# Attention layer of a four-layer graph network: keys on partitions, no row maximum, sums from a product with ones

## The chip, the core and the metric

The kernel runs on one core of a Trainium2 chip. The metric is device time in microseconds (us) of one execution. A core has a matrix engine (PE, whose weight loads are shown as PEld), a vector engine (DVE), an activation engine (ACT), a general engine (POOL), and a queue engine that issues most transfers (SP). Each works through its own list of instructions; semaphores make one wait for another. PE writes to PSUM banks, and DVE or ACT read them from there.

## The reference, cut to what matters

There are 64 graphs of 256 nodes with 256 features, and four layers, each followed by a residual sum and a layer norm. Layer 0 is a recurrence over the nodes of all graphs at once. Layers 1 to 3 work on one graph after the other. Layer 3 is the one that is changed: attention with 8 heads of 32 features, masked by the adjacency matrix.

```python
x = _layernorm(x + L0(x, adj)); x = _layernorm(x + L1(x, adj)); x = _layernorm(x + L2(x, adj))
q = split_heads(x @ Wq + bq)
k = split_heads(x @ Wk + bk)
v = split_heads(x @ Wv + bv)
scores = jnp.einsum('bhqd,bhkd->bhqk', q, k) / np.float32(np.sqrt(HD))
scores = jnp.where(adj[:, None, :, :] > 0, scores, jnp.float32(NEG))
attn = jax.nn.softmax(scores, axis=-1)
out = jnp.einsum('bhqk,bhkd->bhqd', attn, v)
out = out.transpose(0, 2, 1, 3).reshape(b, n, D_OUT)
x = _layernorm(x + out @ Wo + bo)
```

## The kernel before

`_recurrence` computes layer 0 and leaves its result in DRAM (`Hd`). It takes the first 1.6 ms and isn't touched.

`_layers` computes layers 1 to 3. All of a graph's matrices are 256 x 256 and are held as tiles of 128 partitions x 2 x 256 in f32. The class `Graph` has one method for each step. Helpers do the recurring work:

- `flipped` (L923) transposes such a matrix on PE in four 128x128 pieces into a PSUM bank; ACT or DVE copies it out.
- `product` (L933) multiplies two such matrices with four matmuls of 256 columns into a bank.
- `norm_a` (L891) takes mean and variance on DVE (two `bn_stats`, two `bn_aggr`, one add) and the power -0.5 on POOL. Then either `norm_b` (L903) applies them with two DVE operations, or `norm_s` (L910) does it with a small DVE operation for the shift and two ACT operations.
- `row_max` (L950) adds a mask and takes the row's maximum on DVE; `row_exp` (L957) takes the exponential on ACT with that maximum as bias, and the row's sum beside it.

Layer 3 goes: `s3` multiplies queries (stationary) by keys for four heads at once, one half of the heads at a time (`hc` 0 or 1), into four PSUM banks of their own (`sc0` to `sc3`), with queries on partitions. For each head, `max3` and `exp3` make the softmax's numerators, `flip3` transposes them, so that keys lie on partitions, and `pT3` copies them to SBUF. `weights_a` and `weights_b` bring the inverse sums, spread over a head's features, into the same layout by two more transposes. `o3` multiplies by the values, four heads side by side in one bank, and scales with the inverse sums; `f3` is the output product.

The order of the work is written out by hand. In the string `ROUND` (L1197) a step such as `D.flip3.0` calls the method `flip3(0)` of the graph that is in stage D. There are six stages, L, A, B, C, D and E, and a graph moves on by one stage in each round. So a round holds one graph's worth of work, spread over six graphs. The loop at L1209 writes the rounds one after the other, and each engine gets its instructions in that order. Graphs are loaded two rounds ahead on SP. All flips, products and `o3` share a ring of four banks (tag `mm`, L920), taken in turn.

In `ROUND`, flips of attention heads (`D.flip3`) stand between steps that depend on each other, as in `B.xT.2 D.flip3.0 ... B.qk2.0`.

Of the kernel before, what the change touches and what calls it, by code (L numbers as in the profile page):

```python
# [15 lines left out]
NEG = 9000000000000000.0  # L16
EPS = 1e-5
FMAX = 3.0e38
P = 128


# [824 lines left out]
        flush(N - T // 2, N)  # L846


def _layers(tc, ident, Hd, x, adj, w1, b1, l2, l3, out):

# [7 lines left out]
    with ExitStack() as ctx:  # L860
# [9 lines left out]
            _load_col(nc, cols[:, s, :], b)  # L870
        mhalf = const.tile([P, 2], F32, name="mhalf")
        nc.gpsimd.memset(mhalf, -0.5)
        with tc.tile_pool(name="l_setup", bufs=1) as tmp, tc.tile_pool(
            name="l_setup_ps", bufs=2, space=bass.MemoryType.PSUM
        ) as tps:
            _load_wT(nc, tmp, tps, w1, ident, lambda c: W1T[:, :, c * P:(c + 1) * P], "w1")

            bv = tmp.tile([P, 2, P], F32, name="bv3")
            nc.vector.tensor_copy(bv, cols[:, 4, :].unsqueeze(2).to_broadcast([P, 2, P]))
            pb = tps.tile([P, D], F32, tag="wt", name="bv3_ps")  # L880
            for k in range(2):
                nc.tensor.matmul(pb, bv[:, k, :], W3["o"][:, k, :], start=(k == 0), stop=(k == 1))
            nc.vector.tensor_add(b3_r, b3_r, pb)
# [16 lines left out]
            nc.gpsimd.tensor_tensor(rstd, rstd, mhalf, ALU.pow)  # L900
            return mv, rstd

        def norm_b(y, mv, rstd):  # L903
            for c in range(2):
                nc.vector.tensor_scalar(
                    y[:, c, :], y[:, c, :], mv[:, c, 0:1], rstd[:, c:c + 1],
                    ALU.subtract, ALU.mult,
                )

        def norm_s(y, mv, rstd, t):  # L910

            shift = small.tile([P, 2], F32, tag="shift", name=f"shift_{t}")
            nc.vector.scalar_tensor_tensor(shift, mv[:, :, 0], -1.0, rstd, ALU.mult, ALU.mult)  # L913
            for c in range(2):
                nc.scalar.activation(
                    y[:, c, :], y[:, c, :], AF.Identity, bias=shift[:, c:c + 1],
                    scale=rstd[:, c:c + 1],
                )
# [44 lines left out]
        class Graph:  # L963


            def __init__(self, b):
                self.b = b

            def load(self):
                b = self.b  # L970
# [11 lines left out]
            def norm_a(self, l):  # L982
                self.mv = norm_a(self.y, f"{l}_{self.b}")

            def norm_b(self):
                norm_b(self.y, *self.mv)

            def norm_s(self, l):
                norm_s(self.y, *self.mv, f"{l}_{self.b}")


            def degrees_a(self):
# [13 lines left out]

            def adT(self):
                pt = flipped(self.ad, f"ad_{self.b}")
                self.adT_sb = new("adT", self.b)
                for c in range(2):  # L1010
                    nc.scalar.activation(  # L1011
                        self.adT_sb[:, c, :], pt[:, c, :], AF.Copy, scale=self.dis[:, c:c + 1]
                    )
# [21 lines left out]
            def masks(self):  # L1035
                self.neg2 = new("neg2", self.b)
                nc.gpsimd.tensor_scalar(self.neg2, self.ad, -1.0, NEG, ALU.add, ALU.mult)
                self.neg3 = new("neg3", self.b, 4)
                nc.gpsimd.tensor_scalar(self.neg3, self.ad, 0.0, -NEG, ALU.is_le, ALU.mult)

            def qk2(self, s):
                pm = product(W2["qk"[s]], self.xT_sb, f"2{s}_{self.b}")
# [5 lines left out]
            def v2(self):  # L1048
                pm = product(W2["v"], self.xT_sb, f"2v_{self.b}")
                self.vT2 = new("vT2", self.b)  # L1050
                for c in range(2):
                    nc.vector.tensor_scalar(
                        self.vT2[:, c, :], pm[:, c, :], cols[:, 5, c:c + 1], 0.0, ALU.add, ALU.max
                    )

            def w2(self):

                pm = product(self.vT2, W2["o"], f"2w_{self.b}")
                self.w2_sb = new("w2", self.b)
                nc.vector.tensor_copy(self.w2_sb, pm)  # L1060

            def s2(self):
                b = self.b
# [36 lines left out]
                setattr(self, f"qk3{s}", m)  # L1100

            def bias_3(self):
                nc.gpsimd.tensor_add(self.y, self.y, rows(b3_r))  # L1103

            def v3(self):
                pm = product(self.xT_sb, W3["v"], f"3v_{self.b}")
                self.v3_sb = new("v3", self.b)
                nc.vector.tensor_copy(self.v3_sb, pm)
                self.oT3 = new("oT3", self.b)
                self.sm, self.pT = {}, {}  # L1110
                self.mx3 = [None] * 2
                self.sums3 = [None] * 2

            def s3(self, hc):

                self.s_ps = [
                    ps.tile([P, 2, N], F32, tag=f"sc{i}", name=f"s3_{self.b}_{hc}_{i}", bufs=1)
                    for i in range(G)
                ]
                for c in range(2):  # L1120
                    for i in range(G):
                        r = slice(i * HD, (i + 1) * HD)
                        nc.tensor.matmul(  # L1123
                            self.s_ps[i][:, c, :], self.qk30[r, hc, c * P:(c + 1) * P],
                            self.qk31[r, hc, :], start=True, stop=True,
                        )

            def max3(self, h):
                hc, i = divmod(h, G)
                if i == 0:  # L1130
                    self.mx3[hc] = small.tile([P, G, 2], F32, tag="mx3", name=f"mx3_{self.b}_{hc}")
                    self.sums3[hc] = small.tile(
                        [P, 2, G], F32, tag="sums3", name=f"sums3_{self.b}_{hc}"
                    )
                self.sm[h] = new("sm3", f"{self.b}_{h}", 5)
                for c in range(2):
                    row_max(
                        self.sm[h], self.s_ps[i], self.neg3, c, ISQ, self.mx3[hc][:, i, c:c + 1]
                    )

            def exp3(self, h):
                hc, i = divmod(h, G)
                for c in range(2):
                    row_exp(
                        self.sm[h], c, self.mx3[hc][:, i, c:c + 1], self.sums3[hc][:, c, i:i + 1]
                    )

            def flip3(self, h):
                self.pT_ps = flipped(self.sm[h], f"p3_{self.b}_{h}")

            def pT3(self, h):
                self.pT[h] = new("pT3", f"{self.b}_{h}", 8)
                (nc.vector.tensor_copy if h % G == G - 1 else nc.scalar.copy)(  # L1153
                    self.pT[h], self.pT_ps
                )

            def weights_a(self, hc):

                nc.vector.reciprocal(self.sums3[hc], self.sums3[hc])  # L1159
                self.rw = new("rw", f"{self.b}_{hc}", shape=(P, 2, G, HD))  # L1160
                nc.gpsimd.tensor_copy(  # L1161
                    self.rw, self.sums3[hc].unsqueeze(3).to_broadcast([P, 2, G, HD])
                )

            def weights_b(self, hc):
                r_ps = bank(f"tr_r_{self.b}_{hc}", (P, N))
                for c in range(2):
                    nc.tensor.transpose(
                        r_ps[:, c * P:(c + 1) * P], self.rw[:, c].rearrange("p g d -> p (g d)"),
                        ident,  # L1170
                    )
                self.rT = new("rT", f"{self.b}_{hc}", shape=(P, N))
                nc.scalar.copy(self.rT, r_ps)

            def o3(self, hc):

                o_ps = bank(f"o3_{self.b}_{hc}", (P, N))
                for k in range(2):
                    for i in range(G):
                        h = hc * G + i  # L1180
                        nc.tensor.matmul(  # L1181
                            o_ps[i * HD:(i + 1) * HD], self.v3_sb[:, k, h * HD:(h + 1) * HD],
                            self.pT[h][:, k, :], start=(k == 0), stop=(k == 1),
                        )
                nc.vector.tensor_mul(self.oT3[:, hc, :], o_ps, self.rT)

            def f3(self):
                pm = product(self.oT3, W3["o"], f"3f_{self.b}")
# [4 lines left out]

        ROUND = """  # L1197
            B.xT.2 D.flip3.0 D.exp3.1 D.pT3.0 B.qk2.0 D.max3.2 C.norm_a.2 A.norm_s.0 L.residual_0
            D.flip3.1 D.exp3.2 E.weights_b.1 D.pT3.1 E.o3.1 B.qk2.1 D.max3.3 C.norm_b B.masks B.v2
            D.flip3.2 D.exp3.3 D.pT3.2 E.f3 D.s3.1 A.xT.1 D.max3.4 C.xT.3 C.bias_3 E.norm_a.3  # L1200
            D.flip3.3 D.exp3.4 D.pT3.3 B.s2 D.weights_a.0 C.qk3.0 D.max3.5
            D.flip3.4 D.exp3.5 D.pT3.4 D.weights_b.0 A.t C.qk3.1 B.exp2 D.max3.6 E.norm_s.3 E.store L.degrees_a
            D.flip3.5 D.exp3.6 D.pT3.5 D.o3.0 A.g B.w2 D.max3.7 B.pT2 L.norm_a.0 L.degrees_b
            D.flip3.6 D.exp3.7 D.pT3.6 A.norm_a.1 C.v3 C.s3.0 C.max3.0 A.norm_b C.max3.1
            D.flip3.7 C.exp3.0 D.pT3.7 D.weights_a.1 L.adT B.f2
        """.split()
        graphs = [Graph(b) for b in range(B)]
        graphs[0].load()
        for t in range(-1, B + 4):  # L1209
            if 0 <= t + 2 < B:  # L1210
                graphs[t + 2].load()
            for step in ROUND:
                who, name, *args = step.split(".")
                b = t - "LABCDE".index(who) + 1
                if 0 <= b < B:
                    getattr(graphs[b], name)(*map(int, args))


@with_exitstack
def kernel(ctx: ExitStack, tc: tile.TileContext, ins, out):  # L1220
# [14 lines left out]
    l2, l3 = (  # L1235
        {w + n: ins[f"{l}_gnn_{w}{n}"] for w in "Wb" for n in "vkqo"} for l in ("L2", "L3")
    )
    _layers(tc, ident, Hd, x, adj, ins["L1_gnn_W"], ins["L1_gnn_b"], l2, l3, out)


# [34 lines left out]
```

## Time and profile before

| what | value |
|---|---|
| median of 3 runs | 3787.27 us (3783.76 to 3795.49) |
| the profiled execution | 3796.41 us |
| its span, first to last instruction | 3794.7 us |
| mean granted PE clock | 0.976 |
| instructions | 85826 |
| row maxima, L952, DVE | 1152 x 415 to 423 ns |
| exponentials, L959, ACT | 1152 x 502 ns, and as many reads of the sum, 192 ns |
| copies of flipped heads, L1153 | ACT 384 x 573 ns, DVE 128 x 682 ns |
| layer norm by `norm_b`, DVE / by `norm_s`, ACT | 256 x 423 ns / 256 x 593 ns |
| mask for layer 3, L1039, POOL | 1947 ns a graph |

A line of the page's groups reads: source line, engine, operation, output and input by name, sizes, count; then busy time in us, mean ns of one, and the idle time of the engine just before such an instruction, with what ended it. The table of windows gives busy time of each engine for a stretch of the span. The timeline lists instructions by start. The chain of waits follows the last instruction back to what released it, step by step.

### The profile page before, as it was taken

Reading aid. Unit: us, or ns where it says so; the run is one execution under the profiler, and the core shown is the slowest. Engines: PE = TensorE matmul, PEld = TensorE weight load, DVE = VectorE, ACT = ScalarE, POOL = GpSimd, SP = SyncE. Lnnn points to the kernel's source line nnn. Section 1 sums busy time; section 2 is a strip of 40 time slices with the busy share of each in tenths; the row PEclk is TensorE's granted clock in tenths of the full one; section 3 lists DMA queues with packets and bytes.
Section 4 is the critical chain, followed back from the end, with each engine's and each line's share of the span. In section 5 each row is a group of like instructions: output and inputs, shape, how many; then the busy total and the mean of one; then the engine's idle time right before and its main releaser. Section 6 shows DMA issues by size and latency. Waiting matters only on the chain.

```text
span 3794.7 us, 85826 instructions
## 1 busy us (share of the span) xinstructions
PE 3505.6 (92%) x31136; PEld 2546.6 (67%) x31136; DVE 2416.4 (64%) x8777; ACT 2020.5 (53%) x6307; POOL 1672.1 (44%) x1860
## 2 busy tenths in 40 slices
PE   6599999999999989679999999999999999999998
PEld 4355555555555555457777777777777777777776
DVE  1366666676667776446666666666666666666665
ACT  0144444444444444336666666666666666666666
POOL 2266666666667777333233333333333333333331
PEclk9799999999999999979999999999999999999999
DMA  8645575788875642320110011111101111110100
GB/s 286 190 142 137 144 178 133 184 193 200 199 178 148 165 128 74 74 69 26 34 34 29 29 34 34 34 34 34 31 26 34 34 34 34 34 34 26 33 18 15
DMA packets 380448, 331.96 MB, mean 87 GB/s; under 512 B 106220, under 2 KB 354168, under 8 KB 374904
## 3 DMA queue, kind: packets, MB, share of 16 engines
q1 hardware_dynamic: 358064, 307.05, 30.8%
q10 hardware_dynamic: 21960, 19.41, 1.5%
q8 instruction: 247, 4.05, 0.5%
q14 instruction: 177, 1.45, 0.1%
HBM read 224.01 MB, written 82.84 MB: 81 GB/s over the span
## 4 chain that ended last, share of the span: by engine, by line
PE 62%; DVE 20%; POOL 5%; DMA 5%; issue 4%; SPq 2%; ACT 1%; ACTq 0%; DVEq 0%; POOLq 0%
PE mm L938 9%; DVE sm L952 4%; PE rc L580 4%; PE rc L588 4%; PE tr_p L928 4%; PE mm_2v L938 3%; PE o L1181 3%; PE mm_g L938 3%; PE mm_t L938 3%; PE mm_2w L938 3%; PE mm_2s L938 3%; PE mm_3f L938 3%; DVE ACC L613 3%; PE late L504 3%; PE z_ps L580 2%
## 5 line engine op out<-in xcount | busy, mean ns | idle before, releaser
L959 ACT ACTIVATE sm<-sm,mx 128x256 f32<-128x256 f32 x1152 | 573.7, 502 | 165.5 <-DVE mx L952 159.2
L613 DVE SCALAR_TENSOR_TENSOR ACC<-keep,S,ACC 128x128 f32<-128x128 f32 x1712 | 504.4, 345 | 190.2 <-ACT hs L631 176.7
L952 DVE CUSTOM_DVE_ANT_0 sm<-s,neg 128x256 f32<-128x256 f32 x1024 | 386.5, 415 | 24.9 <-PE s L1123 24.9
L649 POOL TENSOR_TENSOR ACC<-ACC,far 128x384 f32<-128x384 f32 (+1 forms) x313 | 371.6, 1187 | 24.5
L928 PE MATMUL tr_p<-ident,sm 128*128 128x128 f32 x2304 | 344.1, 276 | 40.1 <-DVE sums L1159 36.0
L928 PEld LDWEIGHTS tr_p<-ident,sm 128*128 128x128 f32 x2304 | 271.7, 141 | 111.1 <-ACT adT L1011 48.5
L900 POOL TENSOR_TENSOR rstd<-rstd,mhalf 128x2 f32<-128x2 f32 x256 | 178.5, 697 | 357.9 <-DVE shift L913 188.9
L580 PE MATMUL rc<-WxT,xqT 128*64 128x256 f32 x2048 | 328.6, 400 | 1.0 <-issue 1.0
L645 POOL TENSOR_TENSOR far<-hs,S 128x384 f32<-128x384 f32 (+1 forms) x313 | 304.2, 972 | 4.7
L751 POOL TENSOR_TENSOR ready<-ACC,dinv 128x128 f32<-128x128 f32 x255 | 101.9, 400 | 424.8 <-DVE ACC L613 402.1
L1097 ACT ACTIVATE qk<-mm,b_cols 128x256 f32<-128x256 f32 x256 | 107.4, 471 | 267.2 <-PE mm L938 267.2
L1153 ACT COPY pT<-tr_p 128x512 f32<-128x512 f32 x384 | 219.9, 573 | 20.1 <-PE tr_p L928 20.1
L959 ACT ACTIVATION_READ_ACCUMULATOR sm<-sm,mx 128x1 f32 x1152 | 221.7, 192 | 0.0
L896 DVE BATCH_NORM_STATS2 st<-y 128x6 f32<-128x256 f32 x512 | 208.0, 406 | 3.7 <-POOL y L1032 3.6
L1018 ACT COPY xT<-tr_x 128x512 f32<-128x512 f32 x192 | 106.3, 588 | 186.0 <-PE tr_x L928 186.0
L597 ACT COPY xpT<-xpT_ps 128x128 f32<-128x128 f32 x256 | 68.1, 266 | 240.5 <-PE xpT_ps L595 240.5
L1103 POOL TENSOR_TENSOR y<-y,b3o_r 128x512 f32<-128x512 f32 x64 | 81.3, 1270 | 260.6 <-PE tr_x L928 258.8
L588 PE MATMUL rc<-WhT,xpT 128*64 128x128 f32 x2048 | 169.7, 287 | 28.1 <-ACT xpT L597 28.0
L1161 POOL COPY rw<-sums 128x256 f32<-128x256 f32 x128 | 50.7, 396 | 312.3 <-DVE sums L1159 312.1
L588 PEld LDWEIGHTS rc<-WhT,xpT 128*64 128x64 f32 x2048 | 107.4, 137 | 117.4 <-ACT xpT L597 84.2
L1000 POOL TENSOR_TENSOR dis<-dis,mhalf 128x2 f32<-128x2 f32 x64 | 44.2, 690 | 316.7 <-DVE dis L999 316.7
L1032 POOL TENSOR_TENSOR y<-y,g 128x512 f32<-128x512 f32 x64 | 81.4, 1273 | 228.8 <-ACT g L1029 224.4
(161 smaller groups left out, 8565.6 us busy)
## 6 DMA issues: line engine op xcount, KB each, us to landing
xX<-in_x_dram ACTq DMA_DIRECT2D x16, 1024.0 KB
Us<-xu SPq DMA_DIRECT2D x64, 256.0 KB
rows<-in_adj_dram SPq DMA_DIRECT2D x64, 256.0 KB
ACC<-Us SPq DMA_DIRECT2D x32, 512.0 KB
xq<-in_x_dram SPq DMA_DIRECT2D x64, 256.0 KB
Hw<-hs SPq DMA_DIRECT2D x512, 32.0 KB
Es<-eu SPq DMA_DIRECT2D x64, 256.0 KB
early_sb<-Es SPq DMA_DIRECT2D x32, 512.0 KB
```

The costliest lines, as they stand in the source:

```text
L580: nc.tensor.matmul(G[o * B:(o + 1) * B], xqT[a, i // 2][:, i % 2, kc, h * B:(h + 1) * B], WxT[:, kc, o, gates], start=False, stop=False, s ...
L588: nc.tensor.matmul(G[o * B:(o + 1) * B], hT[:, kc * B:(kc + 1) * B], WhT[:, kc, o, g], start=False, stop=(kc == 1), skip_group_check=True,)
L613: nc.vector.scalar_tensor_tensor(acc[:, 0, :], keep[:, j % 2, :], s, acc[:, 0, :], ALU.mult, ALU.add)
L645: nc.gpsimd.tensor_mul(tmp[:, 0:count, :], hs.unsqueeze(1).to_broadcast(shape), s.unsqueeze(2).to_broadcast(shape),)
L649: nc.gpsimd.tensor_add(acc, acc, tmp[:, 0:count, :])
L896: nc.vector.bn_stats(st, y[:, c, :])
L900: nc.gpsimd.tensor_tensor(rstd, rstd, mhalf, ALU.pow)
L928: nc.tensor.transpose(pt[:, a, c * P:(c + 1) * P], src[:, c, a * P:(a + 1) * P], ident)
L938: nc.tensor.matmul(pm[:, c, :], lhsT[:, k, c * P:(c + 1) * P], rhs[:, k, :], start=(k == 0), stop=(k == 1),)
L952: nc.vector.tensor_tensor_reduce(out=dst[:, c, :], in0=src[:, c, :], in1=neg[:, c, :], scale=-scale, scalar=FMAX, op0=ALU.add, op1=ALU.min ...
L959: nc.scalar.activation(dst[:, c, :], dst[:, c, :], AF.Exp, bias=mx, scale=-1.0, accum_out=sums)
L1153: (nc.vector.tensor_copy if h % G == G - 1 else nc.scalar.copy)(self.pT[h], self.pT_ps)
```

## The change

Layer 3 is rewritten from the scores on:

- `s3` makes keys the stationary operand, so the scores lie with keys on partitions, as the product with the values needs them. Then no head is flipped. For this the mask is needed transposed; `adT`, which has the transposed adjacency in PSUM already, makes it (`neg3`) on DVE. It was made by POOL in `masks`.
- The exponential is taken without the row's maximum: for each head DVE adds the mask to both halves at once (128x512), and ACT takes the exponential in place.
- `o3` multiplies the numerators by the values and again by a 128x32 tile of ones, into the other half of the bank. That gives each query's sum, spread over the head's 32 features. DVE inverts the sums (128x256), multiplies, and keeps the largest of sum + 1/sum in `far`.
- After the last graph, the largest of `far` is compared with `LIMIT`; all engines load the outcome and branch. If a sum was out of bounds, `_layer_3` computes the layer once more for all graphs, with the row's maximum. For that, `bias_3` stores the layer's input to DRAM (`Yd`).
- All layer norms are applied on ACT (the former `norm_s` is now `norm_b`). The evacuations of `v2`, `w2` and `v3` move from DVE to ACT.
- `ROUND` is written anew, with five stages and no `D`. `o3.0` is done in stage C and `o3.1` in stage E, one round later.

```diff
+LIMIT = 1.0e20
...
-def _layers(tc, ident, Hd, x, adj, w1, b1, l2, l3, out):
+def _layers(tc, ident, Hd, Yd, x, adj, w1, b1, l2, l3, out):
...
+        ones = const.tile([P, HD], F32, name="ones")
+        nc.gpsimd.memset(ones, 1.0)
+        far = const.tile([P, B, 2], F32, name="far")
...
-        def norm_b(y, mv, rstd):
-            for c in range(2):
-                nc.vector.tensor_scalar(
-                    y[:, c, :], y[:, c, :], mv[:, c, 0:1], rstd[:, c:c + 1],
-                    ALU.subtract, ALU.mult,
-                )
-
-        def norm_s(y, mv, rstd, t):
+        def norm_b(y, mv, rstd, t):
...
             def adT(self):
                 pt = flipped(self.ad, f"ad_{self.b}")
+
+                self.neg3 = new("neg3", self.b, 4)
+                nc.vector.tensor_scalar(self.neg3, pt, 0.0, -NEG, ALU.is_le, ALU.mult)
                 self.adT_sb = new("adT", self.b)
...
                 nc.gpsimd.tensor_scalar(self.neg2, self.ad, -1.0, NEG, ALU.add, ALU.mult)
-                self.neg3 = new("neg3", self.b, 4)
-                nc.gpsimd.tensor_scalar(self.neg3, self.ad, 0.0, -NEG, ALU.is_le, ALU.mult)
...
                 for c in range(2):
-                    nc.vector.tensor_scalar(
-                        self.vT2[:, c, :], pm[:, c, :], cols[:, 5, c:c + 1], 0.0, ALU.add, ALU.max
+                    nc.scalar.activation(
+                        self.vT2[:, c, :], pm[:, c, :], AF.Relu, bias=cols[:, 5, c:c + 1]
                     )
...
-                nc.vector.tensor_copy(self.w2_sb, pm)
+                nc.scalar.copy(self.w2_sb, pm)
...
             def bias_3(self):
+                nc.sync.dma_start(Yd[self.b], self.y)
                 nc.gpsimd.tensor_add(self.y, self.y, rows(b3_r))
...
-                nc.vector.tensor_copy(self.v3_sb, pm)
+                nc.scalar.copy(self.v3_sb, pm)
...
                         nc.tensor.matmul(
-                            self.s_ps[i][:, c, :], self.qk30[r, hc, c * P:(c + 1) * P],
-                            self.qk31[r, hc, :], start=True, stop=True,
+                            s_ps[i][:, c, :], self.qk31[r, hc, c * P:(c + 1) * P],
+                            self.qk30[r, hc, :], start=True, stop=True,
                         )
...
+                self.p = []
+                for i in range(G):
+                    p = new("p3", f"{self.b}_{hc}_{i}", 8)
+                    nc.vector.tensor_add(p, s_ps[i], self.neg3)
+                    nc.scalar.activation(p, p, AF.Exp, scale=ISQ)
+                    self.p.append(p)
+                self.ps_of[hc] = self.p
+
+            def o3(self, hc):
+
+
+                o_ps = bank(f"o3_{self.b}_{hc}")
+                for part in range(2):
+                    for k in range(2):
+                        for i in range(G):
+                            h = hc * G + i
+                            nc.tensor.matmul(
+                                o_ps[i * HD:(i + 1) * HD, part, :],
+                                ones if part else self.v3_sb[:, k, h * HD:(h + 1) * HD],
+                                self.ps_of[hc][i][:, k, :], start=(k == 0), stop=(k == 1),
+                            )
+                rT = new("rT", f"{self.b}_{hc}", shape=(P, N))
+                nc.vector.reciprocal(rT, o_ps[:, 1, :])
+                nc.vector.tensor_mul(self.oT3[:, hc, :], o_ps[:, 0, :], rT)
+                nc.vector.tensor_tensor_reduce(
+                    out=rT, in0=o_ps[:, 1, :], in1=rT, scale=1.0, scalar=0.0, op0=ALU.add,
+                    op1=ALU.max, accum_out=far[:, self.b, hc:hc + 1],
                 )
...
         ROUND = """
...
+            B.xT.2 C.norm_a.2 B.qk2.0 E.o3.1
+            B.qk2.1 C.norm_b.2 E.f3 B.masks L.residual_0
+            A.xT.1 B.v2 C.xT.3 C.bias_3 E.norm_a.3
+            B.s2 C.qk3.0 C.qk3.1 E.norm_b.3 E.store B.exp2
+            C.s3.0 A.t C.v3 B.w2 L.degrees_a
+            B.pT2 C.s3.1 A.g L.norm_a.0 L.degrees_b
+            B.f2 C.o3.0 A.norm_a.1 L.adT A.norm_b.1 L.norm_b.0
         """.split()
...
-        for t in range(-1, B + 4):
+        for t in range(-1, B + 3):
...
-                b = t - "LABCDE".index(who) + 1
+                b = t - "LABCE".index(who) + 1
...
+        flag = small.tile([P, 1], F32, tag="flag", name="flag", bufs=1)
+        nc.vector.tensor_reduce(flag, far.rearrange("p b c -> p (b c)"), AX.X, ALU.max)
+        nc.vector.tensor_scalar(flag, flag, LIMIT, None, ALU.is_gt)
+        count = bank("count", (P, 1))
+        nc.tensor.matmul(count[0:1, :], flag, ones[:, 0:1], start=True, stop=True)
+        found = small.tile([1, 1], mybir.dt.int32, tag="found", name="found", bufs=1)
+        nc.vector.tensor_copy(found, count[0:1, :])
+        return nc.values_load(found)
+
+
+def _layer_3(tc, ident, Yd, adj, l3, out):
...
+        with tc.For_i(0, B, 1) as b:
+            y = work.tile([P, 2, D], F32, name="gy")
+            nc.sync.dma_start(y, Yd[b])
...
+                mx = work.tile([P, 2], F32, tag="gmx", name=f"gmx_{h}")
+                nc.vector.tensor_reduce(mx, sm, AX.X, ALU.max)
...
+                nc.scalar.activation(sm, sm, AF.Exp, scale=1.0 / math.sqrt(HD))
...
+            nc.sync.dma_start(out[b].rearrange("(c p) d -> p c d", p=P), y)
...
-    _layers(tc, ident, Hd, x, adj, ins["L1_gnn_W"], ins["L1_gnn_b"], l2, l3, out)
+    Yd = dram.tile([B, P, 2, D], F32, name="Yd")
+    found = _layers(tc, ident, Hd, Yd, x, adj, ins["L1_gnn_W"], ins["L1_gnn_b"], l2, l3, out)
+    with tc.If(found > 0):
+        _layer_3(tc, ident, Yd, adj, l3, out)
```

The methods `max3`, `exp3`, `flip3`, `pT3`, `weights_a` and `weights_b` and the old `o3` are removed.

## The prediction

> **What bounds the kernel now.** I read the page's first two parts, the table of windows, the chain of waits over one steady period, the groups by form, and the timeline at the start of the layers, in that order.
>
> ```profile
> PE 3505.6 (92%) x31136; PEld 2546.6 (67%) x31136; DVE 2416.4 (64%) x8777; ACT 2020.5 (53%) x6307; POOL 1672.1 (44%) x1860
> PEclk9799999999999999979999999999999999999999
> 2500.00:3000.00 500.00, 488.16 (x3269) 392.42 (x3268) 330.88 (x1266) 322.94 (x961) 159.15 (x180) 1.00 0.11 33
> ```
>
> The last line is one window of 500 us in the layers (PE, PEld, DVE, ACT, POOL busy; clock; DMA): PE 98% busy at full clock, DVE 66%, ACT 65%. In the timeline PE starts the same `s` product at 2798.92 and again at 2832.08 us, so one graph costs 33.16 us, and 64 graphs 2122 us. The rest, mostly the recurrence, is untouched. A PE that is 98% busy looks like the bound. The chain of waits is finer:
>
> ```profile
> 2801.52 1.74 PE mm_2s L938 x8
> ...
> 2809.50 0.44 PE tr_p L928 x4
> 2809.94 1.00 PE o L1181 x16
> ...
> 2814.62 0.69 DVE w L1060
> 2815.32 0.33 DVE sm L952
> 2815.65 0.34 DVE sm L952
> 2816.00 0.08 DVE sums L1080
> 2816.07 0.34 DVE st L896
> ...
> 2820.62 0.33 DVE sm L952
> 2820.96 0.34 DVE sm L952
> ```
>
> (start, length, what). On the chain a product of four matmuls takes 1.73 us of PE, a flip of four transposes 0.44, eight matmuls of `o3` 1.00. From 2814.62 to about 2822 it runs through DVE: even now a long DVE stretch ahead of the next `xT.2` decides. PE stays busy there only because flips and products that don't depend on it are strewn between.
>
> [...]
>
> ```profile
> 1647.91 0.47 PE L928 MATMUL tr_x<-ident,y 128*128 128x128 f32 x1 [5.03 <-DVE y L905]
> ...
> 1650.18 3.78 PE L938 MATMUL mm<-xT,W2q 128*128 128x256 f32 x8 [0.67 <-ACT xT L1018]
> ...
> 1653.76 3.20 PE L938 MATMUL mm<-xT,W2k 128*128 128x256 f32 x8
> ...
> 1656.80 1.89 PE L938 MATMUL mm_2v<-xT,W2v 128*128 128x256 f32 x8
> ```
>
> (start, length, what, in brackets the idle time before and what ended it.) After 5 us of idleness the next products start 3.58 and 3.04 us apart instead of 1.73; the third, 6.6 us on, is at full speed. [...] The trace agrees that it grows far faster per element than other operations:
>
> ```profile
> L1080 DVE RECIPROCAL sums<-sums 128x2 f32<-128x2 f32 x64 | 10.2, 160 | 0.0
> L1159 DVE RECIPROCAL sums<-sums 128x8 f32<-128x8 f32 x128 | 24.9, 195 | 0.0
> L284 DVE RECIPROCAL deg<-deg 128x16 f32<-128x16 f32 x8 | 2.0, 253 | 0.3
> L286 DVE TENSOR_TENSOR deg<-deg,deg 128x16 f32<-128x16 f32 x8 | 1.4, 175 | 0.3
> ```
>
> [...]
>
> **The change, part by part (per graph).** PE loses eight flips (8 x 0.44 = 3.5) and two pairs of transposes of `rw` (2 x 0.22 = 0.4); `o3` doubles to sixteen matmuls a half (+0.85 each, as two more passes of four concurrent ones: the trace's 1.00 less 0.15 of start), +1.7. Net -2.2 us of PE: 12 products x 1.73 + 5 flips x 0.44 + 2 x 1.07 of `s3` + 2 x 1.85 = 28.8 us. That is the floor.
>
> ACT loses 16 exps with accumulator reads (16 x 0.55 = 8.9, two with their reads starting at 2801.64 and ending at 2802.75) and 6 copies (3.4), 2 of `rT` (0.7), and gains eight 128x512 exps. None is in the trace; [...] The nearest row, the 128x512 copy of `xT`, has 588 ns. Two `norm_b` become ACT pairs (1.08 each), `v2`, `w2`, `v3` move there (0.84 + 0.58 + 0.58). About 20 us in all: no bound.
>
> DVE loses 16 `row_max` (16 x 0.43), two copies, `v2`, `w2`, `v3`, two `norm_b`; it gains eight adds of 128x512 out of PSUM (0.69 each as `t`, L1023; 0.61 apart), `neg3` (0.69), two 128x256 `tensor_tensor_reduce` (0.42 + 0.08 read, as L952), and two **reciprocals of 128x256**. From 16 to 256 elements at the 7.25 ns of the last two reciprocal rows gives 1.99 us, [...] I take 2.1. Bounds: 0.42 if it streamed as a copy does[...]. DVE totals about 23 us: no bound either.
>
> The order decides. I follow the queues through one round, 0 being the moment at which ACT ends `A.norm_b.1`, for which `B.xT.2` waits.
> 1. PE flips `xT.2`. On ACT, `L.norm_b.0` (0.98) stands before the copy of `xT` (0.58): `qk2.0` starts at 1.55. Nothing stands between flip and product any more; before, `flip3.0` did.
> 2. `qk2.0` 1.73, `E.o3.1` 1.85: 5.13, DVE sees it at 5.28. Reciprocal 2.1, product with `rT` 0.47: 7.85. `f3`, whose first quarter ran ahead, goes on at 7.92 (`qk2.1` filled PE until 6.9).
> 3. Rest of `f3` 1.30, `xT.1` 0.44, `v2` 1.73, `xT.3` 0.44, `s2`, `qk3.0`, `qk3.1` 3 x 1.73: 17.0. ACT's first half of `qk3.1` +0.7: `s3.0` at 17.7.
> 4. `s3.0` 1.0, `t`, `v3`, `w2` 5.2, `pT2` 0.44: `s3.1` at 24.4. Its first score reaches DVE 1.16 later (`s` to `sm` at 2832.08 and 2833.24), at 25.55.
> 5. DVE now has, in this order: four adds 2.44, `L.norm_a.0` 1.37, `f2` 1.54 (30.9; PE's `g`, `f2` and `o3.0` end at 30.7), reciprocal 2.1, product 0.47, reduce 0.55, and only then `A.norm_a.1` 1.37: 35.4.
> 6. POOL's power 0.75, DVE's shift 0.2; `neg3` (0.69) lies beside the power, but ACT's `adT` pair (0.84), which now waits for DVE, stands ahead of `norm_b.1` (1.0): 37.9. PE has had nothing since the `adT` flip at 31.1.
>
> So a round is 37.9 us at full clock, with 6.8 us of idle PE at its end, a flip, and 1.1 more before the first product. Nothing but transposes runs for 8 us, so I expect the clock to halve in each round. [...] (3.2 in the trace's example: 3.58 + 3.04 - 2 x 1.73); I take 2.55. It falls on `qk2.0` and `o3.1`, which lie on the path. **Round: 40.45 us.**
>
> Moved and hidden: POOL loses `neg3` (1.95) and `rw`. The new `Yd` store (256 KB a graph, DMA 11% busy) is issued on SP after `norm_b.2` and holds POOL's `y + b3` until it lands; behind that stand the powers of `norm_a.3`, needed by ACT only at 18, some 8 us later. If a transfer took longer than that, `exp2` and the exps behind it would be late by the excess; I take none. Scores and tables need no new bank waits: each of the four `mm` banks is free when asked for in the steps above.
>
> The end: one stage fewer, so one partial round fewer. Before, graph 0 is stored at 1751.2 and graph 63 at 3791.5 us; 59 periods after the first is 3708, so the last four rounds took 83 us, some 21 each. The flag, a register load on five engines and the branch: nothing like it in the trace, [...] I take 5. The sums of exps worked out from the reference's inputs lie between 30 and 787, against a limit of 1e20, so the general path isn't entered.
>
> Sum: 64 x (40.45 - 33.16) = 467, - 21, + 5: +451 us on the profiled execution's 3796.4 (span 3794.7). That execution is 9 us above the median shown, so about 4237 us; I say **4235**.
>
> **Rivals.**
> - *PE stays warm.* [...] the bubble may be shorter than I think. Round 37.9: 64 x 4.74 - 16 = +287, 4075 us. For it: flips fill part of the gap; against it: the example above.
> - *The reciprocal streams.* 0.42 us, so 1.7 less at the end and 1.1 at `f3` (PE then bounds there): round 37.65 with a cold clock, +271, 4060 us. Against it: the three rows.
> - *Longer still*: further waits I don't see, for instance the `Yd` transfer being late[...]: from 4340 up.
> - *Faster.* PE is 98% busy, and if the DVE stretch from `s3.1` to `norm_a.1` were hidden, the removed PE work would come back whole: 28.8 plus 2.1 of waits as now (33.16 against a sum of 31.1) gives 30.9, so 64 x 2.26 + 16 = 161 less, 3625 us. The place is step 5. It decides once the idle times of steps 1 to 6 (1.1, 1.0, 0.7, 6.8) sum to under 4.3 us. The order speaks against it: even a free reciprocal leaves the last one near 5.
>
> **How the numbers follow.** Forecast 0.66, warm 0.14, streaming 0.07, longer still 0.07, faster 0.06. The range of 4045 to 4340 takes in the forecast and the next two. All but the last are slower; about 0.3% is what a measurement here tells from no change: faster 0.06, same 0.01, slower 0.93.
>
> **What would show it.** Right: a period near 40 us in the windows; PE waiting at `tr_x` for ACT `y` some 6 to 7 us each round; products of 2q with twice the usual length and PEclk at 8 or so instead of 9; RECIPROCAL 128x256 near 2.1 us; the chain mostly on DVE. Wrong: a period under 33 us; a reciprocal below 0.6 us; no idle PE between the `adT` flip and `xT.2`.

## The result and the profile after

| | us | range |
|---|---|---|
| before, median of 4 | 3785.5 | 3781.3 to 3795.5 |
| after, median of 4 | 4267.1 | 4265.4 to 4271.4 |
| ratio | 1.127 | 95% 1.1245 to 1.1294 |

The changed kernel is 12.7% slower: 482 us by the medians. The general path isn't entered. The first lines are from the page of the kernel after: the engines' busy time, the granted clock in 40 slices, and four of its groups. The last line is a window of 500 us in the layers (busy time of PE, PEld, DVE, ACT, POOL; clock; DMA share; GB/s).

```profile
PE 3592.7 (84%) x30882; PEld 2471.4 (58%) x30882; DVE 2411.0 (57%) x7052; ACT 1833.9 (43%) x4771; POOL 1521.0 (36%) x1669
...
PEclk9899999999999997889888888898888988889889
...
L1130 DVE TENSOR_TENSOR p<-s,neg 128x512 f32<-128x512 f32 x512 | 318.1, 684 | 382.9 <-PE s L1123 382.9
L1149 DVE RECIPROCAL rT<-o 128x256 f32<-128x256 f32 x128 | 224.2, 1752 | 531.5 <-PE o L1143 531.4
L930 PE MATMUL tr_x<-ident,y 128*128 128x128 f32 x768 | 166.2, 333 | 369.0 <-ACT y L917 368.2
...
L1131 ACT ACTIVATE p<-p 128x512 f32<-128x512 f32 x512 | 297.0, 627 | 78.1 <-DVE p L1130 77.9
```

```profile
2500.00:3000.00 500.00, 416.18 (x2608) 306.57 (x2601) 268.84 (x696) 228.94 (x494) 100.00 (x109) 0.88 0.11 34
```

Each engine is busy for less of the time than before: PE is down from 98% to 83%, DVE from 66% to 54%, ACT from 65% to 46%. The clock fell from 1.00 to 0.88. Work was removed and waits were added: 368 us of PE's idle time, 5.75 us a graph, end with ACT's `y`, the normalised input of layer 2.

A graph's period is read off the sum `y` at the end of `f2` (DVE, L1091, once a graph). Its first and last start between 2000 and 3450 us are 2020.8 and 3413.4, 34 periods apart: 40.96 us. Before it was 33.16. The difference of 7.80 times 64 is 499 us. The profiled executions differ by 471.6 (4267.99 and 3796.41), so the ends gave back 28.

The chain of waits of the kernel after, one round of it (start, length, what; pieces of up to 0.02 us are left out):

```profile
2999.84 1.79 DVE p L1130 x3
...
3002.98 0.80 DVE f L1087 x2
3003.80 1.26 DVE y L1091
3005.07 1.68 DVE rT L1149
...
3006.77 0.43 DVE oT L1150
3007.23 0.42 DVE rT L1151
3007.66 0.35 DVE st L905
...
3008.95 0.60 DVE neg L1011
...
3009.58 0.50 ACT adT L1014 x2
...
3010.30 2.07 ACT y L917 x4
3012.38 0.59 ACT xT L1021
...
3013.02 3.78 PE mm L940 x8
3016.80 3.00 PE o L1143 x32
3019.80 1.92 PE mm L940 x8
```

From the adds of `s3.1` to the copy of `xT`, 13 us, the chain holds no PE instruction. On DVE, `f2` (f, y), `o3.0` (rT, oT, rT) and the layer norm of another graph (st) stand one behind the other, though neither `f2` nor `o3.0` is needed by that norm. PE's share of the same stretch, from the timeline (in brackets the idle time before, and what ended it):

```profile
3004.58 0.66 PE L930 MATMUL tr_ad<-ident,ad 128*128 128x128 f32 x4
...
3010.95 1.39 PE L930 MATMUL tr_x<-ident,y 128*128 128x128 f32 x4 [5.72 <-ACT y L917]
...
3013.02 3.78 PE L940 MATMUL mm<-xT,W2q 128*128 128x256 f32 x8 [0.68 <-ACT xT L1021]
...
3016.73 1.94 PE L1143 MATMUL o<-p,v 128*32 128x256 f32 x16
```

PE idles for 5.7 us, flips, and then takes 3.7 us for a product (`qk2.0`) and 3.0 us for `o3.1`, which take 1.93 and 1.86 at full clock in the kernel `filler` below: the clock has halved (granted 0.50 from 3008.84 to 3019.08 us; the window is in the last section). From the start of `qk2.0` to that of `qk2.1` are 6.71 us here and 3.79 in `filler`, so the clock costs 2.92 us a round.

### The profile page after: what moved, and what is told of

It reads as the page before. It is cut to its first block, busy times and chain, and to the rows that moved or that the text cites. A ratio compares the mean times of both kernels' runs of the same rounds, so it can differ in the third digit from the quotient of the medians.

```text
span 4266.3 us, 81884 instructions
## 1 busy us (share of the span) xinstructions
PE 3592.7 (84%) x30882; PEld 2471.4 (58%) x30882; DVE 2411.0 (57%) x7052; ACT 1833.9 (43%) x4771; POOL 1521.0 (36%) x1669
## 3 DMA queue, kind: packets, MB, share of 16 engines
q14 instruction: 154, 1.26, 0.1%
## 4 chain that ended last, share of the span: by engine, by line
PE 60%; DVE 19%; ACT 6%; DMA 5%; issue 4%; POOL 4%; SPq 2%; ACTq 0%; DVEq 0%; POOLq 0%
PE mm L940 14%; PE o L1143 4%; PE rc L581 4%; PE rc L589 4%; DVE p L1130 4%; PE s L1123 3%; ACT y L917 3%; PE mm_3f L940 3%; PE mm_t L940 3%; PE mm_2s L940 3%; PE mm_2v L940 3%; PE mm_2w L940 3%; PE late L505 3%; PE mm_3v L940 3%; DVE rT L1149 3%
## 5 line engine op out<-in xcount | busy, mean ns | idle before, releaser
L1130 DVE TENSOR_TENSOR p<-s,neg 128x512 f32<-128x512 f32 x512 | 318.1, 684 | 382.9 <-PE s L1123 382.9
L1149 DVE RECIPROCAL rT<-o 128x256 f32<-128x256 f32 x128 | 224.2, 1752 | 531.5 <-PE o L1143 531.4
L930 PE MATMUL tr_x<-ident,y 128*128 128x128 f32 x768 | 166.2, 333 | 369.0 <-ACT y L917 368.2
L930 PEld LDWEIGHTS tr_x<-ident,y 128*128 128x128 f32 x768 | 108.5, 163 | 417.0 <-ACT y L917 404.0
L1131 ACT ACTIVATE p<-p 128x512 f32<-128x512 f32 x512 | 297.0, 627 | 78.1 <-DVE p L1130 77.9
L1046 ACT ACTIVATE qk<-mm,b_cols 128x256 f32<-128x256 f32 x256 | 107.3, 470 | 500.8 <-PE mm L940 500.8
L917 ACT ACTIVATE y<-y,shift,rstd 128x256 f32<-128x256 f32 x512 | 271.7, 593 | 28.2 <-DVE shift L915 23.9
L940 PE MATMUL mm<-xT,W2q 128*128 128x256 f32 x512 | 241.6, 653 | 43.2 <-ACT xT L1021 43.2
L1014 ACT ACTIVATE adT<-tr_ad,dis 128x256 f32<-128x256 f32 x128 | 53.6, 470 | 439.9 <-DVE neg L1011 403.4
L940 PEld LDWEIGHTS mm<-xT,W2q 128*128 128x128 f32 x512 | 161.4, 330 | 103.2 <-ACT xT L1021 68.8
L1098 ACT ACTIVATE qk<-mm,b_cols 128x256 f32<-128x256 f32 x256 | 107.3, 470 | 221.5 <-PE mm L940 221.5
```

The lines of the kernel that those rows point to most:

```text
L917: nc.scalar.activation(y[:, c, :], y[:, c, :], AF.Identity, bias=shift[:, c:c + 1], scale=rstd[:, c:c + 1],)
L930: nc.tensor.transpose(pt[:, a, c * P:(c + 1) * P], src[:, c, a * P:(a + 1) * P], ident)
L940: nc.tensor.matmul(pm[:, c, :], lhsT[:, k, c * P:(c + 1) * P], rhs[:, k, :], start=(k == 0), stop=(k == 1),)
L1130: nc.vector.tensor_add(p, s_ps[i], self.neg3)
L1131: nc.scalar.activation(p, p, AF.Exp, scale=ISQ)
L1149: nc.vector.reciprocal(rT, o_ps[:, 1, :])
```

## The experiments

All runs were timed beside the kernel before (medians 3790 to 3796). Times are medians of four; the difference to the kernel after is taken between ratios to the kernel before, since they come from different sets of runs. "Period" is measured as above, "stretch" is the time from the start of `qk2.0` to that of `qk2.1` in the timeline between 2000 and 3450 us. Where only `o3.1` stands between, what exceeds 3.79 is lost to the clock.

| kernel | us | ratio, 95% | period | stretch |
|---|---|---|---|---|
| after | 4267.1 | 1.1245 to 1.1294 | 40.96 | 6.58 to 6.72, mostly 6.71 |
| no_recip | 4117.0 | 1.0844 to 1.0880 | 38.52 | 5.17 to 6.78, mean 5.86 |
| filler | 4102.7 | 1.0802 to 1.0844 | 38.22 | 3.79, in some rounds 5.42 |
| last_row | 4276.6 | 1.1268 to 1.1306 | 40.96 | 5.62 to 5.76, mostly 5.76 |
| no_check | 4203.4 | 1.1050 to 1.1089 | 39.82 | 6.69, 5.31, 6.19 in turn |
| last_row2 | 4060.4 | 1.0687 to 1.0723 | 37.55 | 5.9, with a flip |
| new_order | 3704.6 | 0.9758 to 0.9791 | 31.86 | |
| new_order2 | 3574.1 | 0.9400 to 0.9431 | 29.67 | |
| new2_no_recip | 3569.9 | 0.9380 to 0.9426 | 29.68 | |
| new2_no_ones | 3506.3 | 0.9215 to 0.9258 | 28.58 | |

### The price of the reciprocal

```diff
-                nc.vector.reciprocal(rT, o_ps[:, 1, :])
+                nc.vector.tensor_copy(rT, o_ps[:, 1, :])
```

> The changed kernel with the two 128x256 reciprocals of a graph replaced by copies, so the sums are not inverted. Theory (the order of the round puts DVE work on the path, and the clock halves): a reciprocal takes 1.75 us and a copy about 0.42, so 1.3 us come off the end of each round and up to 0.7 before f3, 2.0 x 64 = 130 us: about 4135 us, with the idle PE and the halved clock still there. Rival (the reciprocals are the price of the change): most of the 480 us come back, below 3900 us.

It measured 4117: 1.127 less 1.086, times 3790, is 155 us. The copy takes 0.42 us, so each reciprocal is 1.33 shorter. The period fell by 2.44. Of that 1.33 are at the end of the round. `f3` takes 1.73 instead of 1.99, 0.26. The clock gives 0.85, since the stretch fell from 6.71 to a mean of 5.86. Together 2.44. So the reciprocal is a third of the loss, partly through the idle time it makes; a kernel without it stays 8.6% slower than before.

### The price of the clock

Twelve matmuls that nobody reads are put where PE idles:

```diff
+            def filler(self):
+                t = ps.tile([P, 2, N], F32, tag="sc0", name=f"filler_{self.b}", bufs=1)
+                for i in range(12):
+                    nc.tensor.matmul(
+                        t[:, i % 2, :], W1T[:, 0, 0:P], W1T[:, 0, :], start=True, stop=True
+                    )
...
-            B.f2 C.o3.0 A.norm_a.1 L.adT A.norm_b.1 L.norm_b.0
+            B.f2 C.o3.0 A.norm_a.1 L.adT A.filler A.norm_b.1 L.norm_b.0
```

> The changed kernel with 12 matmuls of 256 columns, whose results nobody reads, after the adT flip of each round, where PE is idle. Theory: the dependences stay, but the clock stays at full speed, so qk2.0 and o3.1 lose the 3.2 us that they now take more: 64 x 3.2 = 205 us less, about 4060 us, period near 37.7 us. Rival (the slow matmuls lie beside other waits and cost nothing): 4267 us as now, or more if the filler delays the flip.

It measured 4103, by the ratios 169 us less. The window and the timeline of this kernel:

```profile
2500.00:3000.00 500.00, 471.71 (x3087) 364.39 (x3080) 287.47 (x743) 240.34 (x520) 108.79 (x119) 0.99 0.11 35
```

```profile
3006.44 1.99 PE L940 MATMUL mm<-xT,W2q 128*128 128x256 f32 x8 [0.91 <-ACT xT L1028]
3008.37 1.07 PE L1150 MATMUL o<-p,v 128*32 128x256 f32 x16
...
3010.23 1.99 PE L940 MATMUL mm<-xT,W2k 128*128 128x256 f32 x8
```

`qk2.0` is back at 1.99 (starts 1.93 apart) and the stretch at 3.79. The chain is the same otherwise, with added work for PE. So the clock's cost is shown: 2.74 of the 7.80 us a round. It didn't all go: about one round in five still has a stretch of 5.42, 1.63 more, and is longer by as much. A round without loss takes 37.89.

### Moving the norm ahead of `f2` and `o3.0`

```diff
-            B.f2 C.o3.0 A.norm_a.1 L.adT A.norm_b.1 L.norm_b.0
+            A.norm_a.1 A.norm_b.1 B.f2 C.o3.0 L.adT L.norm_b.0
```

> The changed kernel with only the last row of the order changed: A.norm_a.1 and A.norm_b.1 before B.f2, C.o3.0 and L.adT. Every instruction is kept. Theory: norm_a.1 starts when POOL's y sum ends, 3.1 us earlier, and ACT's adT pair (0.8) is no longer ahead of norm_b.1; the idle stretch of PE falls to some 2 us, the clock stays up (3.2 us): 7.1 x 64 = 455 us less, about 3810 us. Rival (the amount of DVE work bounds the round, not its place): within 60 us of 4267.

It measured 4277, no better than the kernel after: a clear miss. The timeline of `last_row` shows why:

```profile
3016.81 0.33 PE L930 MATMUL tr_x<-ident,y 128*128 128x128 f32 x1 [2.39 <-ACT y L917]
...
3017.49 1.75 DVE L1149 RECIPROCAL rT<-o 128x256 f32<-128x256 f32 x1
...
3020.81 0.84 ACT L1014 ACTIVATE adT<-tr_ad,dis 128x256 f32<-128x256 f32 x2 [3.56 <-DVE neg L1011]
...
3022.52 0.58 ACT L1021 COPY xT<-tr_x 128x512 f32<-128x512 f32 x1
...
3023.15 3.78 PE L940 MATMUL mm<-xT,W2q 128*128 128x256 f32 x8 [4.94 <-ACT xT L1021]
```

The flip did move ahead of the reciprocal. But on ACT the copy of `xT` still stands behind `adT`: the flip ends at 3018.20, and the copy starts at 3022.52. ACT is idle for 3.56 us before `adT`, for want of `neg3`, which now waits on DVE behind the reciprocal and the two operations after it. PE's idle time before the flip became idle time after it, and there is more of it: 2.39 and 4.94 us, where the kernel after has 5.72 and 0.68. So a round is 0.95 longer than before the edit at full clock, and the period is the same only because 1.97 instead of 2.92 are lost to the clock (the last section has more on this). Two queues had to be followed, and I had followed one.

`last_row2` takes `adT` and `norm_b.0` out of the way as well, to the row after:

```diff
-            B.xT.2 C.norm_a.2 B.qk2.0 E.o3.1
+            B.xT.2 C.norm_a.2 B.qk2.0 E.o3.1 A.adT A.norm_b.0
...
-            B.f2 C.o3.0 A.norm_a.1 L.adT A.norm_b.1 L.norm_b.0
+            A.norm_a.1 A.norm_b.1 B.f2 C.o3.0
```

> As last_row, and adT and norm_b.0 of the next graph moved behind E.o3.1 of the first row, so that they no longer stand before the copy of xT on ACT. Theory (in last_row the wait only moved from the flip to that copy, which stood on ACT behind adT and norm_b.0, and these behind f2's and o3.0's DVE work): qk2.0 starts some 4.4 us earlier, 64 x 4.4 = 280 us less, about 3990 us with the clock still halved; if the gap is now short enough for the clock to stay, 2.6 us a round more, about 3825 us. Rival (the round is bound by the amount of DVE work or by another wait at its end): above 4150 us.

4060: between the theory (3990) and its rival (4150). The timeline of `last_row2`:

```profile
3013.03 0.33 PE L930 MATMUL tr_x<-ident,y 128*128 128x128 f32 x1 [2.98 <-ACT y L917]
...
3014.74 3.13 PE L940 MATMUL mm<-xT,W2q 128*128 128x256 f32 x8 [0.67 <-ACT xT L1021]
...
3025.01 0.33 PE L930 MATMUL tr_x<-ident,y 128*128 128x128 f32 x1 [0.73 <-ACT y L917]
```

ACT's part of the wait was real: relative to `last_row`, 0.058 of 3790 or 220 us are gone. But in its chain of waits the exps of `s3.1` stand on ACT ahead of the evacuation of `g`, and POOL's sum and the norm follow on that. PE idles for 3 us, and `qk2.0` still runs into the halved clock (3.13 instead of 1.99). The last line is a new wait of 0.73: `xT.1` now stands behind the moved `norm_b.0`. Changing the one row wasn't enough; the next kernels move the norm past whole products.

### What the overflow test costs

`no_check` leaves out the `tensor_tensor_reduce`, the store to `Yd`, the flag, the branch and the general path:

```diff
             def bias_3(self):
-                nc.sync.dma_start(Yd[self.b], self.y)
                 nc.gpsimd.tensor_add(self.y, self.y, rows(b3_r))
...
-                nc.vector.tensor_tensor_reduce(
-                    out=rT, in0=o_ps[:, 1, :], in1=rT, scale=1.0, scalar=0.0, op0=ALU.add,
-                    op1=ALU.max, accum_out=far[:, self.b, hc:hc + 1],
-                )
```

> The changed kernel without the sum's check: no tensor_tensor_reduce in o3, no store of Yd, no flag, no branch and no general path. Theory: one reduce (0.46 us with its read) leaves the DVE stretch at the end of each round, 64 x 0.46 = 30 us, and the end loses some 5 to 8 us: about 4230 us. Rival (the Yd transfers or the branch cost much more): below 4180 us.

4203 was foreseen as about 4230. By the ratios 0.020 of 3790 or 76 us are gone, by the periods 1.14 a round. The reduce explains 0.42 to 0.46. The remainder is in the clock, as the starts of `qk2.0` and `qk2.1` in three rounds that follow each other show:

```profile
2982.13 3.78 PE L940 MATMUL mm<-xT,W2q 128*128 128x256 f32 x8 [0.67 <-ACT xT L1021]
...
2988.82 1.99 PE L940 MATMUL mm<-xT,W2k 128*128 128x256 f32 x8
...
3022.59 3.52 PE L940 MATMUL mm<-xT,W2q 128*128 128x256 f32 x8 [0.68 <-ACT xT L1021]
...
3027.90 1.99 PE L940 MATMUL mm<-xT,W2k 128*128 128x256 f32 x8
```

```profile
3061.65 3.78 PE L940 MATMUL mm<-xT,W2q 128*128 128x256 f32 x8 [0.68 <-ACT xT L1021]
...
3067.84 1.99 PE L940 MATMUL mm<-xT,W2k 128*128 128x256 f32 x8
```

The stretches are 6.69, 5.31 and 6.19, a mean of 6.06, where the kernel after has 6.71 in nearly every round: 0.65 less. With 0.46 that is 1.11 of 1.14. So the test's own work on the path is under half a microsecond a graph, and the rest is a smaller loss to the clock.

### Hiding the whole stretch

`new_order` rewrites all of `ROUND` with the same steps. `o3.0` moves to the next round, `norm_a.1` and `norm_b.1` ahead of both `s3.1` and `f2`, `adT` and `norm_b.0` beside products.

```diff
+            B.xT.2 C.norm_a.2 E.o3.0 B.qk2.0 C.norm_b.2 L.residual_0
+            E.o3.1 B.qk2.1 A.xT.1 B.v2 C.xT.3 C.bias_3 B.masks L.norm_a.0 L.degrees_a
+            E.f3 A.t E.norm_a.3 B.s2 L.norm_b.0 L.degrees_b
+            C.qk3.0 A.g L.adT C.qk3.1 B.exp2 E.norm_b.3 E.store
+            B.w2 A.norm_a.1 C.s3.0 A.norm_b.1 C.v3 B.pT2
+            C.s3.1 B.f2
```

> The changed kernel with all rows of the order rewritten, all instructions kept: o3.0 moves to stage E, t and g come earlier, norm_a.1 lies before the adds of s3.0, and a product or o3 stands between each flip and the product that reads it. Theory: PE's 28.8 us of work a graph plus some 1.5 of waits, 30.3 a round, 64 x 10.6 = 680 us less: about 3590 us, below the kernel before. Rival (the DVE stretch comes back at another place whatever the order): above 3800 us.

3705: 2.2% faster than before, though short of the 3590 expected. The longest wait left in a round is that of `f2` for the copy `pT2`, which on ACT stands behind exps. And one round in four takes 33.12 instead of 31.44 us, which adds 0.42 to the mean period; the granted clock is 0.98 to 0.99 in the windows of 500 us from 2000 to 3500. The wait for `pT2` in the timeline of `new_order`:

```profile
2811.20 1.99 PE L940 MATMUL mm_2f<-w,pT 128*128 128x256 f32 x8 [1.47 <-ACT pT L1080]
```

`new_order2` takes `pT2` ahead of them and closes the round with `xT.2` under `s3.1`:

```diff
-            B.xT.2 C.norm_a.2 E.o3.0 B.qk2.0 C.norm_b.2 L.residual_0
+            C.norm_a.2 E.o3.0 B.qk2.0 C.norm_b.2 L.residual_0
...
-            B.w2 A.norm_a.1 C.s3.0 A.norm_b.1 C.v3 B.pT2
-            C.s3.1 B.f2
+            B.w2 B.pT2 A.norm_a.1 A.norm_b.1 C.s3.0 C.v3 B.f2 A.xT.2 C.s3.1
```

> new_order with the wait of mm_2f for ACT's pT copy (1.5 us a round) taken away: pT2 right behind w2, norm_b.1 before s3.0, f2 and the next xT.2 before s3.1. Every instruction is kept. Theory: PE bounds, and 1.5 to 1.9 us a round come back: about 3600 us. Rival (DVE or ACT bounds by now, so the wait turns up elsewhere): 3680 to 3710 us.

3574: 5.8% faster than before (0.940 to 0.943), 16% less than the kernel after, with the same operations. A window of 1000 us of `new_order2`:

```profile
2500.00:3500.00 1000.00, 997.76 (x7157) 790.11 (x7156) 739.10 (x1918) 611.83 (x1343) 261.94 (x301) 1.00 0.14 44
```

PE is busy for 99.8% of it at full clock. Only now is PE the bound.

Two more kernels start from `new_order2`. In one the reciprocals are again copies; in the other the products with ones are left out (`range(1)` in `o3`, and the reciprocal reads the other half of the bank).

> new_order2 with the two reciprocals of a graph replaced by copies, so the sums are not inverted. Theory (a reciprocal costs only where it stands on the path; in new_order2 PE bounds): within 15 us of new_order2, though 2.7 us of DVE work a round are gone. Rival (the reciprocals cost about the same anywhere): some 150 us less, as they did in the round of the changed kernel.

3570, the same within the intervals (0.938 to 0.943 against 0.940 to 0.943). The reciprocals, worth 155 us in the kernel after, cost nothing once they lie beside PE's work.

> new_order2 without the products with ones, so the sums are not formed (the reciprocal and the reduce read the product with the values). Theory (PE bounds in new_order2): 16 matmuls a round, 2 x 0.87 us of PE, go: 64 x 1.74 = 111 us less, about 3465 us. Rival (DVE or ACT bounds there): within 30 us of new_order2.

3506: 0.0179 of 3795, 68 us, where 111 were expected. The period fell by 1.09 and not by the 1.74 of the matmuls left out. PE's share of the same window is down to 98.5%:

```profile
2500.00:3500.00 1000.00, 985.05 (x6208) 770.93 (x6206) 754.77 (x1954) 613.10 (x1368) 261.97 (x302) 1.00 0.14 43
```

So PE's work decides in `new_order2`, and other waits come close behind it. In the timeline `o3.0` is 0.87 shorter, as expected, but `o3.1` only 0.44, since it now waits for the exponentials (PE's weight loads in `new2_no_ones`):

```profile
2814.73 0.15 PEld L1143 LDWEIGHTS o<-p,v 128*32 128x32 f32 x6 [0.33 <-ACT p L1131]
2815.17 0.57 PEld L1143 LDWEIGHTS o<-p,v 128*32 128x32 f32 x10 [0.29 <-ACT p L1131]
```

Another 0.22 is lost in `v2`, `xT.3` and `f3`; what holds those I didn't separate.

## Why the prediction was right

It gave 4235 with 4045 to 4340 and measured 4267. Its sum, term by term, against the profiled executions:

| term, us | forecast | measured |
|---|---|---|
| round at full clock | 37.9 | 38.04 (40.96 less 2.92); `filler` 37.89 |
| clock, a round | 2.55 | 2.92 |
| round | 40.45 | 40.96 |
| 64 rounds against before | +467 | +499 |
| the ends | -16 | -28 |

The steps can be compared one by one, counted as in the prediction from the end of `norm_b.1` (3011.39 us), with the 2.92 of the clock taken off: the end of `f3` at 9.4 (forecast 9.2), the start of `s3.0` at 17.75 (17.7), of `s3.1` at 24.7 (24.4), the end of `f2`'s `y` at 31.7 (30.9), of `norm_a.1` at 35.6 (35.4), of `norm_b.1` at 38.0 (37.9). So the path was the one foreseen. That its length at full clock is only 0.14 off is in part luck: by the end of `f2` the round was 0.8 late, and the work of DVE from there to the end of `norm_a.1` was 0.6 shorter than forecast.

- **Step 5**, which carried the forecast, held: DVE works through `f2`, reciprocal, product and reduce before `norm_a.1`, and PE runs dry. `new_order2` shows it from the other side: with that order gone, the loss is gone.
- **Step 6** held too: `neg3` and the `adT` pair stand ahead of `norm_b.1`, and `last_row` shows that the pair holds PE just as well where it stands ahead of the copy of `xT`. The idle time was put at 6.8 and measured 5.72. Of the difference 0.44 is that `xT.2` starts at 3010.95 on the first half of `norm_b.1`, whose end (3011.39) I had taken; and the `adT` flip ended 0.8 later than forecast.
- **The reciprocal** was put at 2.1 us, 0.11 more than the prediction's rows give, an excess that no row showed, and took 1.75. Working from the 16-element row to 256 gives (1752 - 253) / 240 = 6.2 ns an element, not the 7.25 of the step from 8 to 16 elements. That made the round shorter by 0.35 at its end.
- **What I didn't see** took it back: `y` of `f2` (L1091) takes 1.26 us instead of 0.69, 0.57 on the path. The last section has what runs beside it.
- **The exp of 128x512** was put at 0.61, which no row showed (the nearest has 588 ns), and averages 0.63. The copies, the adds (0.61 apart) and the doubled `o3` (1.86 a half) are as costed.
- **Step 2** has a slip in what follows from it. PE has the first quarter of `f3` (0.43) to do between 6.9 and 7.92, so the wait at `f3` is 0.6 by the step's own times, not the 1.0 in the list of idle times; and the rival "the reciprocal streams" could gain 0.6 there and not 1.1, which puts it near 4090 instead of 4060. The forecast itself isn't touched. Measured, `f3` takes 1.99 instead of 1.73, a wait of 0.26, with a reciprocal 0.35 shorter. `no_recip` measured 4117.
- **The clock**: the table shows the one term that accounts for most of the miss, 0.37 of 0.51 a round. The clock is at half from 3008.84 to 3019.08; the last 6.1 us of that fall on `qk2.0` and `o3.1`. The 2.55 was shown by no row; the prediction's example from the trace has 3.2. The rival "PE stays warm" had 4075; `filler` measured 4103, with one round in five that still loses 1.63 us.
- **The store to `Yd`** was costed at nothing, and `no_check`, whose 1.14 us a round are the reduce and the clock, leaves next to nothing for it (0.03).
- **The flag and the branch** were put at 5 us without a row to work from. From the issue of the last store to the end of the span are 3.2 us in the kernel before (3791.52 to 3794.7) and 5.7 in the kernel after (4260.61 to 4266.3), 2.5 more.
- **The rival on the other side**, 3625 if the stretch were hidden, named the right place. It needed another order, and the order that does it gives 3574.

## What to carry to other kernels

In these kernels, where the order is written by hand, a ready instruction waited behind one that wasn't ready (in `last_row` the copy of `xT` on ACT, from 3018.20 to 3022.52, with ACT idle until 3020.81), so an operation costs what stands behind it: follow the instruction on the critical path through every queue it passes (here DVE and then ACT), since moving it on one queue only moves the wait. A change that shortens the bounding engine's work and lengthens another engine's stretch needs a new order of the whole round, and its worth can't be read from a version without one: the same operations gave 1.127 and 0.942. When PE starves, read the granted clock too: here 5.72 us of idle PE went with 10.24 us at 0.50, which cost 2.92 us a round. While that lasted, small edits were worth more or less than their own length: `no_check` shortened the period by 1.14 us with at most 0.46 of DVE's path left out, and `last_row` left it as it was with 0.95 more at full clock.

## What the runs showed of the hardware

**A slow sum on DVE beside one on POOL.** Around the slow `y`, the timeline of the kernel after has:

```profile
3003.23 1.29 POOL L1035 TENSOR_TENSOR y<-y,g 128x512 f32<-128x512 f32 x1 [6.06 <-ACT g L1032]
...
3003.80 1.26 DVE L1091 SCALAR_TENSOR_TENSOR y<-f,y 128x512 f32<-128x512 f32 x1
3004.47 1.15 POOL L909 TENSOR_TENSOR rstd<-rstd,mhalf 128x2 f32<-128x2 f32 x1
```

DVE's sum starts while POOL's sum runs and ends 0.54 us after it. Then POOL's power, 0.69 elsewhere, takes 1.15, and ends 0.56 after DVE's sum. In `last_row` POOL's same sum takes 1.28 (3012.42 to 3013.70) and the power behind it 0.70; DVE's sum starts only at 3016.89, and takes 0.69. This sum (L1091, in `filler` L1098) has a median of 1.26 in the kernel after and in `no_recip`, `no_check` and `filler`, which keep the order of `f2` and `norm_a.1`, and 0.69 in all kernels with another order. No kernel changed this overlap alone, so that the one lengthens the other isn't shown.

**Rounds of 40.96 us.** The kernel after and `last_row` have the same period to 0.01 us, 40.96, although without their clock losses (2.92 and 1.97) they differ by 0.95. Once all stages are filled, the rounds of the kernel after (from `qk2.0` to `qk2.0`) come to it step by step: 40.70, 40.83, 40.90, 40.92 and 40.94. Later one round of 41.25 is followed by 40.82, 40.88, 40.93 and 40.94, and in `last_row` one of 41.24 by 40.82, 40.89, 40.92 and 40.95. In the kernel after the granted clock is full for 30.72 us of a round and half for 10.24; near the end of the span it is half for 3.41 (the clock is the third number from the end):

```profile
2978.12:3008.84 30.72, 26.55 (x182) 20.59 (x172) 19.81 (x49) 14.39 (x31) 5.01 (x5) 1.00 0.13 43
3008.84:3019.08 10.24, 7.43 (x36) 4.40 (x40) 2.12 (x9) 4.22 (x9) 3.26 (x4) 0.50 0.01 2
...
4234.24:4237.65 3.41, 3.41 (x10) 2.41 (x9) 1.03 (x5) 1.09 (x2) 0.00 (x0) 0.50 0.23 82
```

So the three lengths are as 9, 3 and 1, and the round is 12 of the shortest. The mean clock is 0.88 in `last_row` too (3000 to 3500 us), and 0.88 in `no_check` (2500 to 3500), whose three periods, 40.45, 39.06 and 39.95, follow each other in turn. What holds two kernels with different work to one period, and why `last_row` loses 0.95 less to the clock, wasn't shown: no run tried it by itself.
